# Attention with a quantized FFN between its pieces: the FFN's input ahead of the hidden rows on VectorE, its load and x1's load moved

## The chip, the cores and the metric

The kernel runs on one core of a Trainium2 chip. The metric is the time of the whole program on the device in microseconds (us). A core has TensorE (PE: matmuls and transposes by matmul), VectorE (DVE), ScalarE (ACT), GpSimd (POOL) and SyncE (SP), which here only issues DMAs. Each engine works through its own instructions in order and waits on semaphores for the others.

## The reference

All data are float32; x is 8 x 1024 x 512.

```python
def fp4_quant_dequant(x):            # blocks of 16 along the last axis
    scale = max(max(abs(block)) / 6, 1e-12)
    q = nearest of (0, .5, 1, 1.5, 2, 3, 4, 6) to abs(block / scale)
    return q * sign * scale

x = x + attention(layernorm(x))      # 16 heads, latent 128, rope, causal softmax
y = fp4(layernorm(x))
h = silu(y @ fp4(w_gate).T) * (y @ fp4(w_up).T)      # 1408 wide
x = x + fp4(h) @ fp4(w_down).T
```

## The kernel before

The attention is cut into 16 units, two per batch element, each of 512 query rows; an odd unit has more keys to go over than the even one before it. For every unit the latent projections are made, then the heads in four groups of four: scores on PE (`sc_ps`), the exponential on ACT (L597), clipping, masking and row sums on DVE and POOL, the sum over values on PE (`num`). The output projection of a unit (`po`, `out_proj`) comes in the next unit; DVE adds x (L772), and the result x1 goes to a DRAM buffer `mid`.

The FFN goes over 64 tiles n of 128 rows of x1. Its weights are quantized and turned once, in the first units. From the fifth unit on (about 553 us) the pieces of the FFN are laid between the steps of the attention, as fillers for PE; the last tiles stand alone at the end (from about 3640 us). For a tile n there are these pieces:

- `fetch(n)`: SP loads x1 into the tile `y` (one buffer).
- `begin(n)`: layernorm statistics (DVE L361 to L363, and a power on POOL), scaling (L367), then `quantize`: block maxima (L254), six small steps for the scales (L259 to L264, in `sc` and `rs`, one buffer each), and for each part of up to 512 columns a multiply (L281), a mask and a step size `m` (L289, L292; one buffer), an add and a subtract (L295) and a multiply (L277).
- `turned(n)`: four transposes of y on PE (L212), and ACT copies the result into `yT` (L214; two buffers).
- `gate(n, k)` and `up(n, k)`, k = 0, 1, 2: matmul groups of 512, 512 and 384 columns. ACT copies the gate into `h` (L142; two buffers) and makes the silu (L819); DVE multiplies by the up part (L831).
- After `up(n, 2)` `quantize` runs over h (1408 columns, three parts), each part ending in a transpose of 32 x 32 blocks (L218). `move_blocks` then issues sixteen DMAs on SP from h to `hT` (L230; one buffer), which finish the transpose.
- `down(n)`: matmuls of hT with the down weights into `pd`, DVE adds x1 (`xr`, in the three buffers of tag `xo`; L881), SP stores the rows. It stands in the program behind `gate(n + 2, 2)`.

The order on PE, DVE, ACT and SP is written out by the kernel itself (`tc.manual_schedule`); that of POOL is left to the scheduler. A planner, `Clock`, keeps an estimated time of PE, DVE and ACT. Work of DVE with no fixed place is queued as jobs with costs in `clk.soon` and `clk.later`; the FFN's quantizations go to `later`, one behind the other. `fill` takes jobs from the queues where DVE has time before its next fixed instruction; `need(key)` lays all jobs up to the last one of that key, just before PE depends on them. So `turned(n)` begins with `need(("y", n))` and `gate(n, 0)` with `need(("h", n - 2))`. Stores and the moves of h are kept back by `send` until the planner's time has come to their data.

The order of a tile's pieces is given by `ffn_pieces`; of before, it reads

```python
for k in range(3):
    yield (3.4, 3.4, 2.6)[k], n, lambda n=n, k=k: gate(n, k)
    if k < 2 and n < last:
        yield 0.0, n + 1, lambda n=n, f=(fetch, begin)[k]: f(n + 1)
```

so y of the next tile is loaded behind `gate(n, 0)` and begun behind `gate(n, 1)`, its jobs behind those of h of tile n - 1 that are still queued.

Of the kernel before, what the change touches and what calls it, by code (L numbers as in the profile page):

```python
# [11 lines left out]
F32 = mybir.dt.float32  # L12
U32 = mybir.dt.uint32
AF = mybir.ActivationFunctionType
ALU = mybir.AluOpType
# [3 lines left out]
P = 128  # L19
B, S, D = 8, 1024, 512  # L20
# [7 lines left out]
NDC = D // P  # L28
NFC = FF // P
BLK = 16  # L30
# [12 lines left out]
def tile_mla_then_fp4_ffn(  # L43
# [30 lines left out]


    ET = mybir.EngineType
    ctx.enter_context(tc.manual_schedule(engines={ET.PE, ET.DVE, ET.Activation, ET.SP}))

    class Clock:

# [18 lines left out]
                job[1]()  # L99

        def lay(self, q):
            cost, run, _, ready = q.popleft()
            self.dve = max(self.dve, ready) + cost
            run()

# [36 lines left out]
        on_act(0.1 + 0.0009 * src.free_size(), lambda: nc.scalar.copy(dst, src))  # L142

    def slack(cost, run, key, soon=False, ready=0.0):
        (clk.soon if soon else clk.later).append((cost, run, key, ready))

    ident = const.tile([P, P], F32, name="ident")
    make_identity(nc, ident)
# [68 lines left out]
    def turn_blocks(part, key, soon=False):  # L217
        slack(0.72, lambda: nc.vector.transpose(part, part), key, soon)  # L218
# [24 lines left out]
    BY_PE = (4 * 2 * B - 1,)  # L243


    def quantize(q, width, key):
        nb = width // BLK
        q3 = q.rearrange("p (b k) -> p b k", k=BLK)
        got = {}

        def amax():
            got["sc"] = sc = p1.tile([P, 88], F32, tag="sc", name="sc")[:, :nb]
            got["rs"] = rs = p1.tile([P, 88], F32, tag="rs", name="rs")[:, :nb]
            nc.vector.tensor_reduce(rs, q3, AX.X, ALU.max, apply_absolute_value=True)  # L254

        def scales():
            sc, rs = got["sc"], got["rs"]

            nc.vector.tensor_scalar(sc, rs, 1.0 / 6.0, None, ALU.mult)  # L259
            nc.vector.scalar_tensor_tensor(rs, sc, -4.0, rs, ALU.mult, ALU.add)  # L260
            nc.vector.scalar_tensor_tensor(rs, sc, -2.0, rs, ALU.mult, ALU.add)
            nc.vector.scalar_tensor_tensor(sc, rs, 1.0 / 6.0, sc, ALU.mult, ALU.add)
            nc.vector.tensor_scalar(sc, sc, 1e-12, None, ALU.max)
            nc.vector.reciprocal(rs, sc)  # L264

        slack(0.06 + 0.0011 * width, amax, key)
        slack(1.1 + 0.008 * nb, scales, key)
        for o in range(0, width, 512):
            step = min(512, width - o)
            part, bl = q[:, o : o + step], slice(o // BLK, (o + step) // BLK)  # L270
            nbl = step // BLK
            part3 = part.rearrange("p (b k) -> p b k", k=BLK)

            def times(which, part3=part3, bl=bl, nbl=nbl):
                by = got[which][:, bl].unsqueeze(2).to_broadcast([P, nbl, BLK])
                if which == "sc":
                    nc.vector.tensor_tensor(part3, part3, by, ALU.mult)  # L277
                else:


                    nc.vector.scalar_tensor_tensor(  # L281
                        part3, part3, BELOW_ONE, by, ALU.mult, ALU.mult
                    )

            def steps(part=part, step=step):
                got["m"] = m = p1.tile([P, 512], F32, tag="m", name="m")[:, :step]
                nc.vector.tensor_scalar(  # L289
                    m.bitcast(U32), part.bitcast(U32), EXP_MASK, None, ALU.bitwise_and  # L290
                )
                nc.vector.tensor_scalar(m, m, 1.0, MAGIC, ALU.max, ALU.mult)  # L292

            def to_grid(op, part=part):
                nc.vector.tensor_tensor(part, part, got["m"], op)  # L295

            pass_cost = 0.06 + 0.00125 * step
            slack(pass_cost, lambda f=times: f("rs"), key)
            slack(1.2 * pass_cost, steps, key)
            slack(pass_cost, lambda f=to_grid: f(ALU.add), key)  # L300
            slack(pass_cost, lambda f=to_grid: f(ALU.subtract), key)
            slack(pass_cost, lambda f=times: f("sc"), key)
            if key[0] == "h" and key[1] not in BY_PE:
                turn_blocks(part, key)


    def weight_pieces():
# [45 lines left out]
    def normed(xt, key):  # L353
        got = {}

        def stats():
            pool, tag = (small, "nx") if key[0] == "x" else (p1, "ny")
            own = pool.tile([P, 10], F32, tag=tag, name=tag)
            st, ve = own[:, 0:6], own[:, 8:9]
            got["mv"], got["rstd"] = mv, rstd = own[:, 6:8], own[:, 9:10]  # L360
            nc.vector.bn_stats(st, xt)  # L361
            nc.vector.bn_aggr(mv, st)
            nc.vector.tensor_scalar(ve, mv[:, 1:2], EPS, None, ALU.add)  # L363
            nc.gpsimd.tensor_tensor(rstd, ve, neg_half, ALU.pow)

        def scaled():
            nc.vector.tensor_scalar(  # L367
                xt, xt, got["mv"][:, 0:1], got["rstd"], ALU.subtract, ALU.mult
            )

        return [(0.9, stats, key), (0.5, scaled, key)]

    def begin_norms(jobs, soon=False):

        parts = [normed(*job) for job in jobs]
        for k in range(2):
            for part in parts:
                slack(*part[k], soon)
# [399 lines left out]


    tiles = [(u, t) for u in range(2 * B) for t in range(NT)]  # L780
    ys, hs, ends = {}, {}, {}

    def fetch(n):
        clk.sent_by_now("store")
        ys[n] = p1.tile([P, D], F32, tag="y", name=f"y_{n}")
        nc.sync.dma_start(out=ys[n], in_=mids[tiles[n]])

    def begin(n):
        begin_norms([(ys[n], ("y", n))])
        quantize(ys[n], D, ("y", n))  # L790

    def hidden(n, w, off, width):
        pg = bank("pg")[:, :width]
# [9 lines left out]

    def turned(n):
        clk.need(("y", n))
        yT = p2.tile([P, NDC, P], F32, tag="yT", name="yT")
        turn(ys[n], yT, NDC)
        ys[n] = yT

# [32 lines left out]
    def hidden_turned(n, done=None):  # L842

        if n in BY_PE:
            return
        if n > 0 and n - 1 not in used:
            waits[n] = clk.dve
            return
        h = hs.pop(n)

        def make():
            clk.sent_by_now("store")
            ends[n] = p3.tile([P, D], F32, tag="xo", name=f"xr_{n}")
            nc.sync.dma_start(out=ends[n], in_=mids.pop(tiles[n]))
            hTs[n] = p1.tile([P, NFC, P], F32, tag="hT", name="hT")
            return hTs[n]

        move_blocks(h, make, ("h", n), clk.dve if n == 0 or done is None else max(done, clk.pe))

    def down(n):  # L860
        clk.need(("h", n))
        if n in BY_PE:
            ends[n] = p3.tile([P, D], F32, tag="xo", name=f"xr_{n}")
            nc.sync.dma_start(out=ends[n], in_=mids.pop(tiles[n]))
            hTs[n] = p1.tile([P, NFC, P], F32, tag="hT", name="hT")
            for off, width in FCH:
                f0, c = off // P, width // P
                turn(hs[n][:, off : off + width], hTs[n][:, f0 : f0 + c, :], c)
            hs.pop(n)
        else:  # L870
            arrived(("h", n))
        hT = hTs[n]
        pd = bank("pd")
        for i in range(NFC):
            mm(pd, lhsT=hT[:, i, :], rhs=wd_T[:, i, :], start=(i == 0), stop=(i == NFC - 1))
        hTs.pop(n)
        used.add(n)
        if n + 1 in waits:
            hidden_turned(n + 1, waits.pop(n + 1))
        xt = ends.pop(n)  # L880
        on_dve(0.7, clk.pe + 0.3, lambda: nc.vector.tensor_tensor(xt, pd, xt, ALU.add))  # L881
        u, t = tiles[n]
        b, rows = rows_of(u, t)
        clk.send(clk.dve, lambda: nc.sync.dma_start(out=out[b, rows, :], in_=xt), "store")

    def ffn_pieces():

        last = len(tiles) - 1
        yield 4.0, 0, lambda: fetch(0)
        yield 10.0, 0, lambda: begin(0)  # L890
        yield 1.0, 0, lambda: turned(0)
        for n in range(last + 1):
            for k in range(3):
                yield (3.4, 3.4, 2.6)[k], n, lambda n=n, k=k: gate(n, k)
                if k < 2 and n < last:
                    yield 0.0, n + 1, lambda n=n, f=(fetch, begin)[k]: f(n + 1)
            if n > 1:
                yield 9.9, n, lambda n=n: down(n - 2)
            for k in range(3):
                yield (3.4, 3.4, 2.6)[k], n, lambda n=n, k=k: up(n, k)  # L900
                if k == 1 and n < last:
                    yield 0.5, n + 1, lambda n=n: turned(n + 1)
        for n in (last - 1, last):
            yield 9.9, last, lambda n=n: down(n)

# [135 lines left out]
```

## Time and profile before

| what | value |
|---|---|
| median of 3 runs | 3835.66 us (3835.64 to 3838.62) |
| the profiled execution, whole | 3835.01 us |
| its span, first to last instruction | 3833.3 us |
| mean granted TensorE clock | 0.974 |
| PE busy | 3559.1 us, 93% |
| DVE busy | 2873.8 us, 75% |
| ACT busy | 1145.5 us, 30% |
| POOL busy | 651.2 us, 17% |
| DVE waits for the loads of x at L772 | 113.4 us |

The profile is of one execution. Busy is the time in which an engine had an instruction under way. A wait is the idle time of an engine before an instruction, put down to the instruction or DMA that came last before it could start. "pt L212 <- DVE y L277" means: the instruction writing pt at line 212 waited for DVE's instruction at line 277, which wrote y. The granted clock is the share of full speed that TensorE was given; in windows of a few us it is near 1 or near 0.5.

### The profile page before, as it was taken

The numbers are of one execution on the slowest core, as the hardware profiler recorded it, in microseconds if no ns is written. First come the engines' busy times: TensorE is split into PE (matmuls) and PEld (weight loads), VectorE is DVE, ScalarE is ACT, GpSimd is POOL, SyncE is SP. The second block draws the span as 40 slices with busy tenths as digits, with TensorE's granted clock in tenths as the row PEclk, the third lists the DMA queues.
The fourth block names the chain that finished last, engine by engine and source line by source line (L and its number), as shares of the span: only waits on it lengthen the run. The fifth ranks groups of instructions, "written<-read, shape, count | busy, mean of one in ns | idle before, by whom it ended". The sixth has DMA issues, their size and how long they took to land. (4 is left out here: it accounts for less than half of the span.)

```text
span 3833.3 us, 45944 instructions
## 1 busy us (share of the span) xinstructions
PE 3559.1 (93%) x17119; PEld 1551.5 (40%) x17119; DVE 2873.8 (75%) x5024; ACT 1145.5 (30%) x1473; POOL 651.2 (17%) x838
## 2 busy tenths in 40 slices
PE   6998989999999998999999999989999999998898
PEld 3333334443444443344434444433444344433343
DVE  5886937777878777777778687776878786777776
ACT  2343433332323222232323233322323222232210
POOL 2233321111111111111111111111211111111100
PEclk9999999999999999999999999999999999999999
DMA  3212211311122211222111222112221113211221
GB/s 76 64 37 69 81 36 30 76 38 38 38 63 46 70 38 32 54 56 69 38 38 38 69 54 59 34 32 70 47 68 31 38 38 75 51 41 29 46 61 40
DMA packets 577038, 192.47 MB, mean 50 GB/s; under 512 B 514864, under 2 KB 515888, under 8 KB 576816
## 3 DMA queue, kind: packets, MB, share of 16 engines
q1 hardware_dynamic: 568512, 187.36, 21.0%
q10 hardware_dynamic: 8304, 2.18, 0.3%
q8 instruction: 136, 2.23, 0.2%
q14 instruction: 86, 0.70, 0.1%
HBM read 94.72 MB, written 33.55 MB: 33 GB/s over the span
## 5 line engine op out<-in xcount | busy, mean ns | idle before, releaser
L597 ACT ACTIVATE pT<-sc_ps 128x1024 f32<-128x1024 f32 (+1 forms) x640 | 566.1, 936 | 1174.6 <-PE sc_ps L129 964.6
L129 PE MATMUL pg<-wu_T,yT 128*128 128x512 f32 (+1 forms) x1536 | 669.2, 584 | 3.8 <-DVE xo L772 3.8
L129 PE MATMUL pg<-wg_T,yT 128*128 128x512 f32 (+1 forms) x1536 | 630.6, 561 | 0.7 <-ACT yT L214 0.7
L129 PE MATMUL pd<-wd_T,hT 128*128 128x512 f32 x1408 | 622.9, 598 | 4.4 <-DVE rs L264 4.4
L615 POOL TENSOR_SCALAR pT<-pT 128x1024 f32<-128x1024 f32 (+1 forms) x320 | 342.1, 1069 | 1065.4 <-ACT pT L597 847.6
L619 POOL TENSOR_SCALAR_AFFINE_SELECT pT<-pT 128x256 f32<-128x256 f32 (+1 forms) x384 | 233.4, 608 | 1462.6 <-DVE pT L612 1184.0
L641 DVE TENSOR_TENSOR pT<-pT 128x1024 f32<-128x1024 f32 (+3 forms) x528 | 472.7, 920 | 3.9 <-POOL pT L619 0.6
L129 PEld LDWEIGHTS pg<-wu_T,yT 128*128 128x128 f32 x1536 | 296.9, 200 | 333.9 <-issue 274.4
L129 PEld LDWEIGHTS pg<-wg_T,yT 128*128 128x128 f32 x1536 | 288.8, 190 | 326.1 <-issue 248.9
L129 PEld LDWEIGHTS pd<-wd_T,hT 128*128 128x128 f32 x1408 | 266.3, 191 | 345.5 <-issue 327.6
L612 DVE TENSOR_SCALAR pT<-pT 128x1024 f32<-128x1024 f32 (+1 forms) x320 | 205.0, 641 | 248.0 <-ACT pT L597 246.9
L129 PE MATMUL sc_ps<-qc,kT 32*128 32x512 f32 (+3 forms) x3072 | 343.5, 532 | 9.1 <-ACT pT L597 9.0
L129 PE MATMUL num<-pT,v 128*32 128x512 f32 (+3 forms) x3072 | 326.1, 501 | 5.6 <-POOL pT L619 5.2
L129 PE MATMUL sc_ps<-qr,kr 32*128 32x512 f32 (+3 forms) x3072 | 309.8, 488 | 4.2 <-DVE qr L533 4.2
L142 ACT COPY h<-pg 128x512 f32<-128x512 f32 (+1 forms) x192 | 105.7, 551 | 609.3 <-PE pg L129 580.6
L831 DVE TENSOR_TENSOR h<-pg,h 128x512 f32<-128x512 f32 (+1 forms) x192 | 123.1, 642 | 218.8 <-PE pg L129 208.3
L295 DVE TENSOR_TENSOR h<-h,m 128x512 f32<-128x512 f32 (+1 forms) x384 | 257.3, 670 | 11.8
L129 PE MATMUL po<-wo,aT 128*128 128x512 f32 x512 | 226.2, 600 | 30.9 <-DMA wo<-in_w_o_dram 27.9
L129 PEld LDWEIGHTS sc_ps<-qc,kT 32*128 32x128 f32 x3072 | 115.9, 186 | 226.8 <-issue 154.8
L212 PE MATMUL pt<-ident,y 128*128 128x128 f32 x256 | 48.2, 319 | 168.5 <-DVE y L277 158.1
L772 DVE TENSOR_TENSOR xo<-po,xo 128x512 f32<-128x512 f32 x64 | 44.1, 688 | 202.5 <-DMA xo<-in_x_dram 113.4
L129 PEld LDWEIGHTS sc_ps<-qr,kr 32*128 32x128 f32 x3072 | 147.3, 188 | 109.9 <-issue 85.5
(103 smaller groups left out, 3473.3 us busy)
## 6 DMA issues: line engine op xcount, KB each, us to landing
hT<-h SPq DMA_DIRECT2D x1008, 44.0 KB, 2.1
xo<-in_x_dram SPq DMA_DIRECT2D x64, 256.0 KB, 2.9
wo<-in_w_o_dram SPq DMA_DIRECT2D x16, 1024.0 KB, 5.2
mid<-xo SPq DMA_DIRECT2D x64, 256.0 KB, 2.8
y<-mid SPq DMA_DIRECT2D x64, 256.0 KB, 2.7
xr<-mid SPq DMA_DIRECT2D x64, 256.0 KB, 2.8
out_dram<-xr SPq DMA_DIRECT2D x64, 256.0 KB, 2.0
xp<-in_x_dram SPq DMA_DIRECT2D x30, 512.0 KB, 4.0
```

What stands on the lines that cost most here:

```text
L129: nc.tensor.matmul(dst, **kw)
L142: on_act(0.1 + 0.0009 * src.free_size(), lambda: nc.scalar.copy(dst, src))
L212: nc.tensor.transpose(pt[:, i, :], src[:, i * P : (i + 1) * P], ident)
L295: nc.vector.tensor_tensor(part, part, got["m"], op)
L597: lambda: nc.scalar.activation(part, sc[:, 2 * k : 2 * k + 2, :cols], AF.Exp, scale=SM_SCALE),
L612: lambda: nc.vector.tensor_scalar(part, part, E_HI, E_LO, ALU.min, ALU.max),
L615: nc.gpsimd.tensor_scalar(part, part, E_HI, E_LO, ALU.min, ALU.max)
L619: nc.gpsimd.affine_select(out=diag, in_=diag, pattern=[[0, 2], [0, len(segs)], [1, P]], compare_op=ALU.is_ge, fill=0.0, base=0, channel_mu ...
L641: lambda a=whole, b=part: nc.vector.tensor_tensor(a, a, b, ALU.add),
L772: on_dve(0.7, clk.pe + 0.3, lambda: nc.vector.tensor_tensor(xt, po, xt, ALU.add))
L831: lambda: nc.vector.tensor_tensor(h, pg, h, ALU.mult),
```

## The change

SP is no longer among the engines whose order is written out; the scheduler orders its DMAs. A job carries a flag that says whether others may be put in front of it (not where `m` is in use by the job before). `begin(n)` puts y's jobs in front of the first such job in `clk.later`, that is ahead of what is left of the hidden rows of earlier tiles, and y's scales are kept in the first columns of `yT`, which is now allocated there, in place of `sc` and `rs`. `begin(n + 1)` follows `gate(n, 0)` instead of `gate(n, 1)`; `fetch(n + 2)` follows `turned(n + 1)`, ahead of `up(n, 2)`, where before `fetch(n + 2)` stood behind `gate(n + 1, 0)`. `turned` also moves the planner's time of PE up to that of DVE. x1's load for the last add moves from the front of the sixteen DMAs of h into `down(n)`.

```diff
-    ctx.enter_context(tc.manual_schedule(engines={ET.PE, ET.DVE, ET.Activation, ET.SP}))
+    ctx.enter_context(tc.manual_schedule(engines={ET.PE, ET.DVE, ET.Activation}))
...
+    def ahead_of_rows(jobs):
+        q = clk.later
+        at = next((i for i, x in enumerate(q) if x[4]), len(q))
+        for job in reversed(jobs):
+            q.insert(at, (*job, 0.0, True))
...
-    def quantize(q, width, key):
+    def quantize_jobs(q, width, key, scales_in):
...
         def amax():
-            got["sc"] = sc = p1.tile([P, 88], F32, tag="sc", name="sc")[:, :nb]
-            got["rs"] = rs = p1.tile([P, 88], F32, tag="rs", name="rs")[:, :nb]
+            got["sc"], got["rs"] = sc, rs = scales_in()
...
+            jobs.append((pass_cost, lambda f=times: f("rs"), key, True))
+            jobs.append((1.2 * pass_cost, steps, key, True))
+            jobs.append((pass_cost, lambda f=to_grid: f(ALU.add), key, False))
+            jobs.append((pass_cost, lambda f=to_grid: f(ALU.subtract), key, False))
+            jobs.append((pass_cost, lambda f=times: f("sc"), key, True))
             if key[0] == "h" and key[1] not in BY_PE:
-                turn_blocks(part, key)
+                jobs.append((0.72, lambda p=part: nc.vector.transpose(p, p), key, True))
+        return jobs
...
     def begin(n):
-        begin_norms([(ys[n], ("y", n))])
-        quantize(ys[n], D, ("y", n))
+        yTs[n] = yT = p2.tile([P, NDC, P], F32, tag="yT", name="yT")
+        jobs = normed(ys[n], ("y", n))
+        scales_in = lambda: (yT[:, 0, : D // BLK], yT[:, 1, : D // BLK])
+        jobs += [x[:3] for x in quantize_jobs(ys[n], D, ("y", n), scales_in)]
+        ahead_of_rows(jobs)
...
     def turned(n):
         clk.need(("y", n))
-        yT = p2.tile([P, NDC, P], F32, tag="yT", name="yT")
+        clk.pe = max(clk.pe, clk.dve)
+        yT = yTs.pop(n)
...
         def make():
-            clk.sent_by_now("store")
-            ends[n] = p3.tile([P, D], F32, tag="xo", name=f"xr_{n}")
-            nc.sync.dma_start(out=ends[n], in_=mids.pop(tiles[n]))
             hTs[n] = p1.tile([P, NFC, P], F32, tag="hT", name="hT")
...
     def down(n):
         clk.need(("h", n))
+        clk.sent_by_now("store")
+        ends[n] = p3.tile([P, D], F32, tag="xo", name=f"xr_{n}")
+        nc.sync.dma_start(out=ends[n], in_=mids.pop(tiles[n]))
...
         yield 1.0, 0, lambda: turned(0)
+        yield 0.0, 1, lambda: fetch(1)
         for n in range(last + 1):
             for k in range(3):
                 yield (3.4, 3.4, 2.6)[k], n, lambda n=n, k=k: gate(n, k)
-                if k < 2 and n < last:
-                    yield 0.0, n + 1, lambda n=n, f=(fetch, begin)[k]: f(n + 1)
+                if k == 0 and n < last:
+                    yield 0.0, n + 1, lambda n=n: begin(n + 1)
...
                 if k == 1 and n < last:
                     yield 0.5, n + 1, lambda n=n: turned(n + 1)
+                    if n + 1 < last:
+                        yield 0.0, n + 2, lambda n=n: fetch(n + 2)
```

More of the change, by code (lines that the diff above doesn't have):

```diff
@@ L101, in lay @@
         def lay(self, q):
-            cost, run, _, ready = q.popleft()
+            cost, run, _, ready, _ = q.popleft()
             self.dve = max(self.dve, ready) + cost
@@ L144, in slack @@
     def slack(cost, run, key, soon=False, ready=0.0):
-        (clk.soon if soon else clk.later).append((cost, run, key, ready))
+        (clk.soon if soon else clk.later).append((cost, run, key, ready, True))
+    def ahead_of_rows(jobs):
[3 more added lines that the diff above has]
+            q.insert(at, (*job, 0.0, True))
     ident = const.tile([P, P], F32, name="ident")
@@ L243, in tile_mla_then_fp4_ffn @@
     BY_PE = (4 * 2 * B - 1,)
-    def quantize(q, width, key):
+    def quantize_jobs(q, width, key, scales_in):
         nb = width // BLK
         q3 = q.rearrange("p (b k) -> p b k", k=BLK)
-        got = {}
+        got, jobs = {}, []
         def amax():
-            got["sc"] = sc = p1.tile([P, 88], F32, tag="sc", name="sc")[:, :nb]
-            got["rs"] = rs = p1.tile([P, 88], F32, tag="rs", name="rs")[:, :nb]
+            got["sc"], got["rs"] = sc, rs = scales_in()
             nc.vector.tensor_reduce(rs, q3, AX.X, ALU.max, apply_absolute_value=True)
@@ L264, in scales @@
             nc.vector.reciprocal(rs, sc)
-        slack(0.06 + 0.0011 * width, amax, key)
-        slack(1.1 + 0.008 * nb, scales, key)
+        jobs.append((0.06 + 0.0011 * width, amax, key, True))
+        jobs.append((1.1 + 0.008 * nb, scales, key, True))
         for o in range(0, width, 512):
@@ L297, in quantize, with own @@
             pass_cost = 0.06 + 0.00125 * step
[L298 to L302, printed above, removed]
-            if key[0] == "h" and key[1] not in BY_PE:
-                turn_blocks(part, key)
+            jobs.append((pass_cost, lambda f=times: f("rs"), key, True))
[3 more added lines that the diff above has]
+            jobs.append((pass_cost, lambda f=times: f("sc"), key, True))
+            if key[0] == "h" and key[1] not in BY_PE:
+                jobs.append((0.72, lambda p=part: nc.vector.transpose(p, p), key, True))
+        return jobs
+    def quantize(q, width, key):
+        def own():
+            return [p1.tile([P, 88], F32, tag=x, name=x)[:, : width // BLK] for x in ("sc", "rs")]
+        for cost, run, k, free in quantize_jobs(q, width, key, own):
+            clk.later.append((cost, run, k, 0.0, free))
     def weight_pieces():
@@ L780, in tile_mla_then_fp4_ffn @@
     tiles = [(u, t) for u in range(2 * B) for t in range(NT)]
-    ys, hs, ends = {}, {}, {}
+    ys, yTs, hs, ends = {}, {}, {}, {}
     def fetch(n):
@@ L861, in down @@
         clk.need(("h", n))
+        clk.sent_by_now("store")
+        ends[n] = p3.tile([P, D], F32, tag="xo", name=f"xr_{n}")
+        nc.sync.dma_start(out=ends[n], in_=mids.pop(tiles[n]))
         if n in BY_PE:
-            ends[n] = p3.tile([P, D], F32, tag="xo", name=f"xr_{n}")
-            nc.sync.dma_start(out=ends[n], in_=mids.pop(tiles[n]))
             hTs[n] = p1.tile([P, NFC, P], F32, tag="hT", name="hT")
```

## The prediction

> **What bounds the kernel now.** I read the engines' busy time first, then TensorE's waits, then the stretch around one of its stalls on VectorE, TensorE, SyncE and ScalarE, and last the granted clock around a stall.
>
> The page's first part says which engine sets the time (busy us, share, instructions):
>
> ```profile
> span 3833.3 us, 45944 instructions
> PE 3559.1 (93%) x17119; PEld 1551.5 (40%) x17119; DVE 2873.8 (75%) x5024; ACT 1145.5 (30%) x1473; POOL 651.2 (17%) x838
> ```
>
> TensorE is busy 93% of the span and has some 270 us without work. That is all a new order can win, apart from clock. What it waits for (engine, line, releaser: total us, times, longest):
>
> ```profile
> PE pt L212 <- DVE y L277: 158.1, 40, 10.0
> PE po L129 <- DMA wo<-in_w_o_dram: 27.9, 8, 8.6
> ...
> PE pt L212 <- DVE xo L772: 10.4, 6, 2.6
> ...
> PE pv L129 <- DVE xr L881: 6.0, 5, 1.2
> PE pd L129 <- DVE rs L264: 4.4, 1, 4.4
> PE pg L129 <- DVE xo L772: 3.8, 4, 1.7
> ```
>
> Well over half of the idle time is one wait: the four transposes of an FFN input y need the last step of y's quantization (L277). By gaps of 0.8 us and more it is 156.5 us in 37 gaps; six gaps come back in every pair of attention units (a period of 522 us, five of them): 1.9, 5.7, 2.2, 7.4, 2.3 and 2.2 us, and the last tiles have 10.0, 6.3, 4.3, 7.3 and 2.2. The other lines are small.
>
> One of them, the 7.4 us, on VectorE, TensorE, SyncE and ScalarE (start, us, line, operation; the idle time before it in brackets):
>
> ```profile
> 1978.14 0.58 DVE L218 STREAM_TRANSPOSE h<-h 128x384 f32<-128x384 f32 x1
> ...
> 1981.94 0.68 DVE L361 BATCH_NORM_STATS2 ny<-y 128x6 f32<-128x512 f32 x1
> ...
> 1990.13 0.69 DVE L277 TENSOR_TENSOR y<-y,sc 128x512 f32<-128x512 f32 x1
> ```
> ```profile
> 1976.57 7.03 PE L129 MATMUL pg<-wu_T,yT 128*128 128x512 f32 x16
> 1990.97 1.08 PE L212 MATMUL pt<-ident,y 128*128 128x128 f32 x4 [7.37 <-DVE y L277]
> ```
> ```profile
> 1978.87 10.49 SPq L230 DMA_DIRECT2D hT<-h  x16
> 1992.09 0.33 SPq L786 DMA_DIRECT2D y<-mid  x1
> ```
> ```profile
> 2003.47 0.59 ACT L142 COPY h<-pg 128x512 f32<-128x512 f32 x1 [6.97 <-PE pg L129]
> ```
>
> VectorE never stood idle for long here. It finished the quantization of the previous h first, its last transpose ending at 1978.7, and only then began y, which took 1981.94 to 1990.82: 8.9 us, 0.7 of them a multiply of the path, so **y costs 8.2 us**. TensorE ended at 1983.6. SyncE started h's sixteen small DMAs at once and took 10.5 us to issue them; the last lands 2.1 us later by the page's DMA part, at about 1991.5. The copy that needs that h's buffer (two exist) starts at 2003.47, so **12 us were spare behind h** and none before y.
>
> **The change, part by part.** The program has as many instructions on each engine as before. TensorE's order is the same up to its 7893rd of 8769, and shifts in small pieces from tile 54 on. So the price is in waits.
>
> *y before the rows of h.* y's jobs enter the queue ahead of the previous tile's h, one matmul group (3.5 us at 16 per 7.03 us) earlier, with scales in a buffer of their own, so no wait for sc and rs. Following the built order tile by tile, with the durations of the rows, y comes too late on 40 tiles by 173 us in the order of before (156.5 were measured, so this way of counting is about 10% heavy), and in the changed order on one: tile 0, with 9.6 us, which has nothing earlier to go to. Every other tile has at least 16.9 us to spare. Gain: 156.5 - 9.6 = **147 us**. No cover is needed for that; the y that was late is simply not last. The bounds are 130 and 150.
>
> *The load of y a group sooner and x1's load beside down.* VectorE waits 113.4 us in all for x loads at L772, and TensorE 10.4 + 3.8 us behind that. With the x1 loads out of the way of the sixteen h DMAs these shrink, and I take the two TensorE rows, cut to 13.5 us by the same gap limit, as gone: **-13.5** (0 to -14). y's load is late by 4.4 us once per pair, hidden in the 16.9 us. x1's load takes 0.42 us of issue and 2.8 to land, and down's eleven weight tiles run about 9.7 us (622.9 us over 64 tiles), so it is covered; uncovered it would cost 64 x 3.2 = 205 us, but only on VectorE's last add, which no matmul needs but for its bank.
>
> *What is late next: h.* y's 8.2 us now stand before the rows of h. Those cost, per tile: maxima 1.6, scales 1.9, two wide parts of 0.69 + 0.51 + 0.54 + 2 x 0.70 + 0.76 + 0.71 = 4.6 each, one narrow part 3.6: 16.3 us. Behind them is the move: from the last transpose's end to the landing it took 12 to 12.7 us (10.5 to 11.4 of issue and 2.1). Only then may ScalarE copy gate(n+2, 0) into that h buffer, and it is in order: the exponentials of the attention, and so scores, are queued behind that copy. Counted along the built order with a move of 12.0 us, hT of tile n lands after gate(n+2, 0) is ready in six of ten tiles per pair, by 13.3, 7.3, 8.2, 6.0, 4.4 and 1.2 us. TensorE has work that does not need ScalarE for 4.3, 8.5, 6.1, 6.4, 8.3 and 7.6 us in those places; what is left is 9.0 + 0 + 2.1 + 0 + 0 + 0 = 11.1 us per pair, 55.5 in five. Tile 0 adds 13.9 - 8.3 = 5.6. In the end, without attention between, the loop is 8.2 + 16.3 + 12.0 us and some 3 us of multiplies and adds of the path, 39 to 40, against 30 us of TensorE work per tile; it is 6 to 13 us late on seven tiles and TensorE covers 5 to 7 of each: 23 us. Sum: 55.5 + 5.6 + 23 = **+84 us**. Before, ScalarE waited for hT 19.3 us in three places, all in the tail, and on the path it never did, so this wait is not shown by the trace at its new size. Lower bound 30 (only the tail and part of one tile per pair), upper bound 190 (4 us more per tile; one unlucky wait can do that, since SyncE itself was up to 14.5 us late with such a move in places). I take the count, as the move's duration is a measured one.
>
> *Other waits of the new VectorE order.* krp at L452 (0.4 us each) is found behind y on one group in each pair, **+13.5** in all (0 to 25). w_o's load is 4.8 us late per pair instead of 3.3: **+5** (0 to 40).
>
> *SyncE's order left to the scheduler.* In the built order the sixteen DMAs stand at most 0.6 us behind their transposes, where before they were held back 2.7 to 14.5 us on five tiles of the first pair; that is already in the numbers above. Stores move back, and nothing waits for them but their buffer. Taken as nothing beyond w_o; its price where it fails is a rival.
>
> *The clock.* A gap costs more than its length (columns: window, us; busy us and instructions of PE, PEld, DVE, ACT, POOL; granted clock; DMA share; GB/s):
>
> ```profile
> 1038.00:1042.30 4.30, 2.21 (x6) 0.66 (x4) 4.30 (x6) 0.00 (x0) 3.16 (x3) 1.00 0.14 21
> 1043.50:1047.00 3.50, 3.50 (x7) 1.68 (x5) 0.00 (x0) 0.14 (x1) 0.00 (x0) 0.51 0.65 225
> 1047.00:1050.40 3.40, 3.40 (x43) 1.81 (x43) 2.74 (x3) 1.51 (x2) 0.00 (x0) 1.00 0.00 0
> ```
>
> After a gap of 2.2 us the clock is 0.51 for 3.5 us, then full again. After the first 500 us TensorE is busy for 108 us at half clock, so 54 us are lost, over about 50 gaps: 1.1 us each. 42 gaps (37 + 5) go, some 24 come (two per pair, tile 0, seven in the tail, krp): 18 x 1.1 = **-20 us** (0 to -35). The Trainium skill ("TensorE: Matmul & The Clock Gate", "Part 1: The HAM clock gate") puts the half rate behind an idle window of about 3.4 us; the 2.2 us gap above speaks against this. By that rule the short gaps would have cost no clock, and the term would be an estimated -13, the sum -71.
>
> **Sum**, on the profiled execution (3835.0 us: the span of 3833.3 and 1.7 around it, 0.65 below the median): -147 - 13.5 + 84 + 13.5 + 5 - 20 = -78, that is **3757 us**.
>
> **Rivals.**
> *(1) Slower: the move of h becomes the bound.* Same mechanism as the +84, 4 us later on each tile that is late: then three more tiles per pair pass TensorE's cover and the stalls are 189 us instead of 84, with the clock's gain down to 5. 3835 + (-147 - 13.5 + 189 + 13.5 + 5 - 5) = **3877**. It turns the sign from about 3 us more per move (160 us of stalls eat the whole gain). For it: sixteen issues in a row of 10.5 to 11.4 us, and spare time of 6.8 to 17.5 us behind typical tiles, less than y's 8.2 for some. Against: the count already takes the slowest chain of each tile, and ran 10% heavy on the y waits. Chance 0.25.
> *(2) Slower: SyncE's order delays w_o or x.* If w_o comes 10 us later in each of the 11 units from 5 on, 110 us take the place of the 5: **3862**. For it: w_o's wait is 27.9 us already and its load goes behind everything issued before. Against: outside the first 550 us the row is only 13.7 us. Chance 0.06.
> *(3) Much faster: h's move is covered.* If ScalarE's copies wait but TensorE's scores always have a bank, -147 - 13.5 + 13.5 + 5 - 35 = -177: **3658**. For it: VectorE is 75% busy and waits 113 us for x alone. Against: ScalarE waits 6 to 7 us for hT in the tail even before. Chance 0.11.
> *(4) No difference within what a measurement can tell from none* (0.2%, 7.7 us): the stalls come out near 160. This is the border between the forecast and (1), chance 0.08.
>
> **How the numbers follow.** The forecast has 0.50; with (3), faster 0.61; (4) gives same 0.08; (1) and (2) give slower 0.31. The range reaches from 3685 (stalls near the lower bound of 30, clock -35) to 3882 (a little over rival 1): what lies under it is most of (3), above it the far end of (1). For the forecast alone it is 3715 to 3800.
>
> **What would show it.** Right: TensorE's wait for y at L277 falls to about 10 us in one place; the wait of ScalarE's copy L142 for hT rises from 19 us to over 100; the period of a pair goes from 522 to about 511 us; the granted clock rises above 0.974; VectorE's x waits shrink well below 113 us. Wrong: y still waits in many places (the reordering does not do what it says); TensorE idles behind ScalarE or hT for over 160 us; w_o's row grows beyond 40 us.

## The result, and the profile after

The changed kernel takes 3769.56 us (median of 4 runs, 3762.56 to 3771.3) against 3836.0 us: a ratio of 0.9822 (95% interval 0.9805 to 0.9839), 66 us less. The profiled execution took 3769.9 us. The profile's first part of the changed kernel:

```profile
span 3768.2 us, 45975 instructions
PE 3550.3 (94%) x17119; PEld 1550.3 (41%) x17119; DVE 2852.6 (76%) x5024; ACT 1136.8 (30%) x1473; POOL 669.8 (18%) x838
```

The span is 65.1 us shorter. TensorE's time without work (span less busy) fell from 274.2 to 217.9 us, and its busy time by 8.8 us with the same 17119 instructions, with the granted clock at 0.976 for 0.974. What TensorE now waits for:

```profile
PE pqr L129 <- ACT h L142: 41.9, 5, 9.0
PE sc_ps L129 <- ACT pT L612: 24.9, 22, 7.8
PE po L129 <- DMA wo<-in_w_o_dram: 24.5, 5, 13.2
...
PE pp L129 <- ACT h L142: 13.5, 5, 3.1
PE pp L129 <- DVE krp L467: 11.4, 6, 3.8
PE num L129 <- POOL pT L634: 11.2, 14, 1.5
PE pt L219 <- DVE y L284: 9.7, 1, 9.7
PE po L129 <- DVE aT L717: 8.5, 2, 4.3
```

The wait for y went from 158.1 us in 40 places to 9.7 in one. The new head of the list is ScalarE's copy of the gate into h. What that copy waits for is in ScalarE's waits, where the row was 19.3 us before:

```profile
ACT h L142 <- DMA hT<-h: 415.0, 31, 25.9
```

One place of the 41.9 us, once in every pair of units, on TensorE, ScalarE, SyncE and VectorE of the changed kernel:

```profile
1375.82 2.08 PE L129 MATMUL pqr<-cq,wqr 128*128 128x512 f32 x2 [8.32 <-ACT h L142]
```
```profile
1375.18 0.59 ACT L142 COPY h<-pg 128x512 f32<-128x512 f32 x1 [17.82 <-DMA hT<-h]
```
```profile
1362.98 10.51 SPq L237 DMA_DIRECT2D hT<-h  x16
```
```profile
1336.87 0.69 DVE L284 TENSOR_TENSOR y<-y,yT 128x512 f32<-128x512 f32 x1
...
1362.34 0.58 DVE L311 STREAM_TRANSPOSE h<-h 128x384 f32<-128x384 f32 x1
```

y was complete at 1337.6, h's last transpose only at 1362.9; sixteen issues and the landing took until 1375, and the copy that needs that buffer stood 17.8 us in ScalarE's order, TensorE 8.3 us behind it.

### The profile page after: what moved, and what is told of

It reads as the page before. It is cut to its first block, busy times and chain, and to the rows that moved or that the text cites. A ratio compares the mean times of both kernels' runs of the same rounds, so it can differ in the third digit from the quotient of the medians.

```text
span 3768.2 us, 45975 instructions
## 1 busy us (share of the span) xinstructions
PE 3550.3 (94%) x17119; PEld 1550.3 (41%) x17119; DVE 2852.6 (76%) x5024; ACT 1136.8 (30%) x1473; POOL 669.8 (18%) x838
## 4 chain that ended last, share of the span: by engine, by line
PE 58%; DVE 14%; SPq 6%; issue 3%; DMA 2%; ACT 2%; POOL 1%; DVEq 0%; ACTq 0%; POOLq 0%
PE pg L129 21%; PE pd L129 11%; PE sc_ps L129 8%; SPq L237 6%; PE po L129 5%; PE num L129 4%; PE pp L129 2%; DVE h L302 2%; DVE pT L656 2%; PE den L129 1%; DVE h L311 1%; DVE h L284 1%; DMA hT<-h 1%; PE pv L129 1%; PE pqr L129 1%
## 5 line engine op out<-in xcount | busy, mean ns | idle before, releaser
L129 PE MATMUL pg<-wg_T,yT 128*128 128x512 f32 (+1 forms) x1536 | 641.7, 569 | 2.4 <-ACT h L142 1.7
L129 PE MATMUL pg<-wu_T,yT 128*128 128x512 f32 (+1 forms) x1536 | 638.9, 562 | 0.0
L630 POOL TENSOR_SCALAR pT<-pT 128x1024 f32<-128x1024 f32 (+1 forms) x320 | 351.3, 1098 | 1049.1 <-ACT pT L612 677.4
L656 DVE TENSOR_TENSOR pT<-pT 128x1024 f32<-128x1024 f32 (+3 forms) x528 | 463.7, 904 | 3.7 <-POOL pT L634 0.6
L129 PEld LDWEIGHTS pg<-wu_T,yT 128*128 128x128 f32 x1536 | 282.6, 190 | 315.7 <-issue 248.7
L129 PE MATMUL sc_ps<-qc,kT 32*128 32x512 f32 (+3 forms) x3072 | 342.4, 530 | 25.0 <-ACT pT L612 24.9
L129 PE MATMUL num<-pT,v 128*32 128x512 f32 (+3 forms) x3072 | 327.8, 499 | 11.8 <-POOL pT L634 11.2
L129 PE MATMUL po<-wo,aT 128*128 128x512 f32 x512 | 236.5, 622 | 36.6 <-DMA wo<-in_w_o_dram 24.5
L302 DVE TENSOR_TENSOR h<-h,m 128x512 f32<-128x512 f32 (+1 forms) x384 | 260.1, 677 | 10.7
L129 PEld LDWEIGHTS po<-wo,aT 128*128 128x128 f32 x512 | 101.5, 200 | 169.2 <-issue 121.8
L129 PEld LDWEIGHTS num<-pT,v 128*32 128x32 f32 x3072 | 67.9, 108 | 224.8 <-issue 132.3
```

The source lines that it names most:

```text
L129: nc.tensor.matmul(dst, **kw)
L630: nc.gpsimd.tensor_scalar(part, part, E_HI, E_LO, ALU.min, ALU.max)
L656: lambda a=whole, b=part: nc.vector.tensor_tensor(a, a, b, ALU.add),
```

## The experiments

They ask which part of the change gives the gain, and what the wait for h costs. The theory going in (A) was the prediction's: the place in front of the rows of h gives nearly all, the move of h takes half of it back. Times are medians of four runs; the ratio is to the kernel before on the same chip.

**y_first_alone.** The kernel before with y's jobs in front, their scales in `yT`, and the change's line in `turned`; loads, places and SyncE's order are as before.

```diff
+        ahead_of_rows(jobs)          # y's jobs, scales in yT
```

> Kernel before with only y's jobs put in front of the rows of h (and y's scales in yT); pieces, x1's load and SyncE's order as before. Theory A (the order on VectorE carries nearly all the gain, the move of h the loss): TensorE's wait for y at L284 (L277 of before) falls from 158 to under 25 us, ScalarE's wait for hT rises to some hundred us, time 3755 to 3800. Theory B (the earlier load and start, or SyncE's free order, carry the gain): y still waits for over 80 us, time 3815 or more.

3888.51 us, ratio 1.0131 (1.0116 to 1.0147): slower than before. Neither theory gave this: TensorE's wait for y is 9.6 us, as A said, and the time is in B's range. VectorE's own waits show a row that before had not, and TensorE's have these, the first of which is 11.2 us in the changed kernel, where the second is missing:

```profile
DVE ny L376 <- DMA y<-mid: 175.9, 19, 12.5
```
```profile
PE num L129 <- POOL pT L634: 41.2, 19, 6.3
PE pg L129 <- DVE xr L901: 30.4, 6, 5.9
```

With y in front and its load still behind the sixteen DMAs of h, VectorE stands in order before y's statistics, and its later work with it. What TensorE loses by that is not h: its stalls behind the copies into h are 66 us here and 64 in the changed kernel. It is the rows behind xr (55 us for 7.5) and behind POOL's part of the attention, and the clock (TensorE's busy time is 3592.0 us for 3550.3). So the front place, without the rest of the change, is a loss.

**no_front.** The changed kernel without the front place:

```diff
-        ahead_of_rows(jobs)
+        for job in jobs:
+            clk.later.append((*job, 0.0, True))
```

> Changed kernel, but y's jobs go to the end of VectorE's queue, behind the rows of h, as before; the earlier load and start, x1's load beside down and SyncE's free order stay. Theory A: the y wait is back at 110 to 160 us, ScalarE's wait for hT falls below 100 us, time 3810 to 3850. Theory B: the y wait stays under 50 us, time 3755 to 3795.

3747.09 us, ratio 0.9764 (0.9747 to 0.978), 22 us *faster* than the changed kernel. That is under theory B's range, and A fell with it. TensorE's wait for y:

```profile
PE pt L219 <- DVE y L284: 96.1, 24, 9.6
```

62 of the 158 us of y's wait are gone without any change of order between y and h, and ScalarE has no row for hT. The same place as above, in no_front:

```profile
1359.42 1.12 PE L219 MATMUL pt<-ident,y 128*128 128x128 f32 x4 [5.70 <-DVE y L284]
```
```profile
1338.92 10.51 SPq L237 DMA_DIRECT2D hT<-h  x16
```

Here h's move starts some 22 us earlier in the program's course than above (24 on the clock; ScalarE's copy of qc lies at 1353.8 here and at 1356.3 there) and nobody waits for it; y is late by 5.7 us. In the changed kernel y is in time and h costs 8.3. VectorE is short by 6 to 8 us at this point of the pair, and the order only chooses who pays. From here on I had a theory H in place of A: the earlier start of y carries the gain (early_alone below says how far that held); the front place moves VectorE's shortage from y to h, where it is paid through the move.

**plain4.** The changed kernel with a shorter move, four DMAs in place of sixteen; it leaves out the exchange of the 32 x 32 blocks:

```diff
-                for q in range(4):
-                    nc.sync.dma_start(
-                        out=dst[32 * q : 32 * q + 32, :, 32 * g : 32 * g + 32],
-                        in_=src4[32 * g : 32 * g + 32, q])
+                nc.sync.dma_start(
+                    out=dst[32 * g : 32 * g + 32].rearrange("p n k -> p (n k)"),
+                    in_=src[32 * g : 32 * g + 32])
```

> Changed kernel with the move of h done by four plain DMAs in place of sixteen: same bytes, same place in the order, but the exchange of the 32 x 32 blocks is left out. The move takes about 5 us instead of 12. Theory A (the loss is h's lateness by its move): six of ten tiles land 7 us earlier, only one per pair is still late by 2 us beyond TensorE's cover, stalls behind ScalarE's copy of h fall from some 80 to 10 to 20 us, time 3690 to 3712. Theory C (the stalls come from VectorE's own order, the move is only the last in the chain's record): they stay over 55 us, time 3745 or more.

3642.85 us, ratio 0.9492 (0.9478 to 0.9507): 127 us under the changed kernel, some 50 more than A's range. TensorE's busy time and its wait behind the copy into h:

```profile
PE 3517.4 (97%) x17119; PEld 1536.1 (42%) x17119; DVE 2855.2 (78%) x5024; ACT 1140.6 (31%) x1473; POOL 665.6 (18%) x838
```

```profile
PE pqr L129 <- ACT h L142: 10.0, 5, 2.4
```

The copy's wait did fall as A said. What was left out of the expectation: the waits for krp (11.4 to 3.8 us) and aT went too (that they were late behind the same stalls is likely, not shown), and TensorE's busy time fell by 33 us with the clock at 0.988.

**move_plus.** The changed kernel with six DMAs of each move issued twice:

```diff
+            if key[0] == "h":
+                for q in range(6):
+                    nc.sync.dma_start(... the block (q % 4, 3) again ...)
```

> Changed kernel with six of the sixteen DMAs of each move issued twice, to the same places with the same data: each move 3.7 to 4.3 us longer. Theory A (the slower rival of the prediction priced it): stalls behind hT rise by about 105 us and the clock loses some 10, time 3850 to 3890. Theory C: TensorE's other work covers it, time below 3800.

3962.52 us, ratio 1.0328 (1.0313 to 1.0344): 193 us more than the changed kernel, where some 100 was expected. In the profiles TensorE lost 151 us more to idleness and 39.5 us more to the clock (busy 3589.8 for 3550.3). With plain4 this prices a microsecond of the move: about 18 us of time per us taken off (127 for some 7), some 48 per us put on (193 for 4).

**no_front_plain4.** The two edits of no_front and plain4 together.

> As no_front (y behind the rows of h), with the move of h by four plain DMAs, the exchange of the 32 x 32 blocks left out. Theory H (with y in front VectorE's shortage falls on h and is paid through the move; with y behind it falls on y, and the move has slack): the edit that gave 127 us in the changed kernel gives little here, time 3725 to 3750, y's wait stays at 85 to 100 us. If the move's length is a cost in any order (DMA queues, SyncE): below 3700.

3746.54 us, ratio 0.9758 (0.9744 to 0.9773): no difference to no_front's 3747.09; the y wait is 96.2 us. The edit that gave 127 us with y in front gives nothing with y behind. H holds: the length of the move is a cost only because of the front place.

**act_half.** A shorter move that computes everything:

```diff
-                    nc.sync.dma_start(
+                    (nc.scalar if key[0] == "h" and q in (1, 3) else nc.sync).dma_start(
```

> Changed kernel with eight of the sixteen DMAs of each move issued by ScalarE instead of SyncE, the same work, the result complete. The move takes about 7 us instead of 12 if the issues run side by side; ScalarE pays about 5 us of issue per tile and may stand waiting for the transposes. Theory A (the move's length is the loss): stalls behind hT fall to 20 to 50 us, time 3680 to 3740. If ScalarE's wait in its order costs more than the shorter move gives: 3770 or more.

3764.11 us, ratio 0.9805 (0.9788 to 0.9821), the same as the changed kernel within the intervals, and between the two expectations. The two queues did work side by side (5.3 us of issue on SyncE, 5.6 on ScalarE, from the same moment), and TensorE's row of 41.9 us fell to 18.8. But ScalarE now stands before its own DMAs for the transposes: its waits "<- DMA hT<-h" before exponentials and copies of the attention come to some 300 us, and on TensorE the rows of pv (24.1 us for 7.5), of pg (29 for 2.4) and of po behind w_o (39.7 for 24.5) grew.

**sp_manual, late_places, xr_early.** Three parts of the change undone, one at a time, in the changed kernel:

```diff
# sp_manual
-    ctx.enter_context(tc.manual_schedule(engines={ET.PE, ET.DVE, ET.Activation}))
+    ctx.enter_context(tc.manual_schedule(engines={ET.PE, ET.DVE, ET.Activation, ET.SP}))
# late_places: fetch(n + 1) behind gate(n, 0), begin(n + 1) behind gate(n, 1)
# xr_early: xr's load in make(), in front of the sixteen DMAs
```

> Changed kernel with SyncE's order written by the planner again; all else as changed. Theory D (SyncE's free order starts h's move right behind its transposes): the moves start later by up to 14 us in places, ScalarE's wait for hT (415 us) and TensorE's stalls behind it grow, time 3790 to 3840. Theory E (with the loads placed earlier the written order is as good): 3760 to 3780.

3804.92 us, ratio 0.9912 (0.9897 to 0.9927): 35 us slower than with the free order. The way expected for it was wrong, though: ScalarE's wait for hT did not grow (380 us for 415). The row that grew is another (11.2 us with the free order):

```profile
PE num L129 <- POOL pT L634: 37.4, 20, 5.7
```

Why POOL gets late with SyncE's written order was not tried.

> Changed kernel with the load and the start of y back at their places of before (load behind gate(n, 0), start behind gate(n, 1)); y still in front of the rows of h, SyncE free, x1's load beside down. Theory F (y in front needs the earlier load, or VectorE stands before y's statistics and h with it): VectorE's wait for y's load rises from 38 us to over 100, time 3800 to 3890. Theory G (what made y_first_alone slow is SyncE's written order alone): that wait stays under 60 us, time 3755 to 3785.

3769.37 us, ratio 0.9816 (0.9801 to 0.9831): no change. VectorE's wait for y's load is 45.2 us (38.5 in the changed kernel). So F falls: with SyncE free and y in front, the earlier places add nothing. G holds in this much, that the free order, with x1's load in `down(n)`, takes away what made y_first_alone slow. The written order alone did not make it so: sp_manual has that order too, with the earlier places and x1's load in `down(n)`, and there the wait is 63.6 us instead of 175.9 and the time 84 us less. Which of those two helps there was not tried.

> Changed kernel with x1's load back in front of the sixteen DMAs of h. Theory D: in SyncE's order that load, and its wait for a free buffer of tag xo, can hold up the move; h later by 0.5 to 3 us on late tiles, time 3770 to 3830. If x1's load has no part in it: 3760 to 3775.

3769.97 us, ratio 0.9821 (0.9802 to 0.984): no change. With SyncE free, where x1's load stands does not matter.

**sp_free_alone and early_alone.** The two candidates for the gain, without the front place: the kernel before with SyncE free, and the changed kernel with neither the front place nor SyncE free.

> Kernel before with only SyncE's order left to the scheduler. If that order by itself gives much of the gain: TensorE's waits behind xo at L772 (14 us) go and VectorE's wait for x (113 us) falls below 50, y's wait (158 us) falls below 130, time 3790 to 3815. If it helps only beside the earlier pieces: y's wait stays at 150 or more, time 3820 to 3840.

> Changed kernel with y's jobs behind the rows of h and SyncE's order written by the planner: what is left of the change is the earlier load and start of y and x1's load beside down. If the earlier start carries the gain of the kernel without the front place (92 us): y's wait 90 to 110 us, time 3750 to 3785. If it is the free order: y's wait over 130 us, time 3800 to 3835.

sp_free_alone: 3818.67 us, ratio 0.9949 (0.9932 to 0.9965). early_alone: 3744.79 us, ratio 0.9757 (0.9743 to 0.9772), as fast as no_front. The y wait of the first and of the second:

```profile
PE pt L212 <- DVE y L277: 158.2, 40, 10.0
```
```profile
PE pt L219 <- DVE y L284: 96.0, 24, 9.6
```

The free order alone gives 18 us and leaves y's wait; TensorE's waits behind xo (14 us) are what went. In early_alone they went too (1.0 us left), and there the free order gives nothing more (no_front). So what else the change holds gives 92 us alone. That is a bundle: the earlier load and start of y, x1's load in `down(n)`, the scales in `yT`, and the line in `turned` that moves the planner's time of PE.

Within it, the earlier start is not what TensorE gained by in the five pairs, where some 45 of the 62 us lie (107.7 to 62.2). One place where the wait went, with h's last transpose and the start of y on VectorE and y's transposes on TensorE, first in the kernel before, then in early_alone:

```profile
1406.46 0.57 DVE L218 STREAM_TRANSPOSE h<-h 128x384 f32<-128x384 f32 x1
1406.95 0.65 DVE L361 BATCH_NORM_STATS2 ny<-y 128x6 f32<-128x512 f32 x1
```
```profile
1417.89 0.66 PE L212 MATMUL pt<-ident,y 128*128 128x128 f32 x4 [2.19 <-DVE y L277]
```
```profile
1381.49 0.58 DVE L311 STREAM_TRANSPOSE h<-h 128x384 f32<-128x384 f32 x1
1381.99 0.65 DVE L376 BATCH_NORM_STATS2 ny<-y 128x6 f32<-128x512 f32 x1
```
```profile
1398.97 0.60 PE L219 MATMUL pt<-ident,y 128*128 128x128 f32 x4
```

In both, y begins at the end of h's last transpose, and its load was issued long before that (36 and 27 us); the kernel before has no wait of VectorE for that load at all. What came sooner is h: y's transposes on TensorE start 11.4 us after that last transpose in the kernel before, with a wait of 2.2 us, and 17.5 us after it in early_alone, with none. VectorE took up h's rows earlier, ahead of fixed work of the attention. This is what the line in `turned` does: the planner's PE is later, so `fill` sees more time before the next fixed instruction and lays more jobs there. Read off the programs, and not run: early_alone without this line has VectorE's order of the kernel before from tile 2 to tile 53, and with the line but y's load and start at their old places it keeps its own there. In the last tiles, with some 17 of the 62 us, the line and the places both change the order, and their shares were not taken apart. So the first half of H was right in that the gain needs no front place, and wrong in its cause.

**front_some.** What H points to: y in front only where, in the traces of no_front and of the changed kernel, y's lateness costs more than h's.

```diff
-        ahead_of_rows(jobs)
+        if n == 2 or (n < 54 and n % 10 in (8, 0)):
+            ahead_of_rows(jobs)
+        else:
+            for job in jobs:
+                clk.later.append((*job, 0.0, True))
```

> Changed kernel with y in front of the rows of h only at tile 2 and, up to tile 53, at those tiles of each ten where y was later without it than h is with it (the 8th and 0th), elsewhere behind. Theory H: the y waits left are the 5.7 us ones per pair, tile 0 and the end, some 52 us; stalls behind h 10 to 20 us; time 3710 to 3740, below both kernels and no_front (3747). If one place in front disturbs its neighbours: 3745 to 3770.

3721.38 us, ratio 0.9697 (0.9682 to 0.9711), the fastest kernel that computes everything: 116 us under the kernel before on its chip, 48 under the changed one.

```profile
PE pt L219 <- DVE y L284: 53.3, 13, 9.6
PE pp L129 <- ACT h L142: 15.3, 5, 4.3
```

y's wait is what was expected; the wait behind h came back in one place per pair. The choice fits this kernel's period of ten tiles and no other.

## Why the prediction came out, point by point

The time (3757 forecast, 3769.6 measured) and most terms held, and so did the signs that the prediction named: a pair takes some 510 us for 522 (511 forecast). The reasons given for two terms did not hold, and the clock was mis-sized. Rows without a term took some 9 us, the largest TensorE's num behind POOL (5.2 to 11.2 us).

*y, -147.* Measured -148.4 (158.1 to 9.7), with tile 0 left as said. But the prediction gave it all to the order in front of h. The runs split it: the rest of the change takes 62 us at no price, some 45 of them by where the planner lays the rows of h; the front place takes the other 86 and is the sole reason for the next term. The line in `turned` had no term in the prediction, and the term came out near all the same because with y in front y is in time, whichever part is credited with it.

*h, +84.* Stalls behind the copy and hT: 41.9 + 13.5 + 5.3 + 2.0 + 1.7 in the rows of "ACT h", and 15.9 more of sc_ps behind ScalarE than before (24.9 less 9.0), 80 us. The place was right too: ScalarE's copy in its order, two places per pair (8.1 to 9.0 and 2.3 to 3.1 us, where 9.0 and 2.1 stood). The step that failed is the one that was not taken: the prediction set +84 against -147 as prices of the whole change, and never set the front place's own 86 against its own 80, plus krp and clock. Done so, the front place is a loss, which no_front shows by 22 us.

*x and x1, -13.5.* The rows of TensorE behind xo did go. The cause given, x1's load out of the way, is not needed for it: xr_early puts it back without effect, and sp_free_alone removes the rows alone. Under SyncE's written order it may still be the cause, as early_alone, which has that order, is rid of the rows too. VectorE's wait for x fell from 113.4 to 26.4 us, as said it would, but in early_alone it is still 101.2 and the time is 92 us down: that wait was no measure of the gain.

*krp, +13.5 and w_o, +5.* krp measured +11.4. po's rows (w_o, aT, h and rc together) went from 30.9 to 36.6 us: +5.7, though of w_o's load itself nothing (27.9 to 24.5).

*SyncE's order, taken as nothing.* Alone it is worth 18 us, with the front place 35, with the rest of the change but not the front place nothing. That it should cost (rival 2) was not seen in any run.

*The clock, -20.* Measured -8.8. It was counted by gaps: 18 fewer at 1.1 us each. By the same limit of 0.8 us there were 14 fewer after the first 500 us (58 to 44), and the price per gap does not hold: no_front has 24 fewer and gains 10.7 us of busy time, plain4 36 fewer and gains 41.7. Around the 8.3 us gap shown above (window, us; busy of PE, PEld, DVE, ACT, POOL; granted clock; DMA share; GB/s):

```profile
1372.00:1375.80 3.80, 0.00 (x0) 0.00 (x0) 0.00 (x0) 0.62 (x2) 0.00 (x0) 0.50 0.44 65
1377.00:1381.00 4.00, 4.00 (x6) 1.52 (x5) 3.56 (x7) 0.74 (x2) 2.86 (x4) 0.50 0.32 50
1381.00:1384.50 3.50, 3.50 (x11) 1.79 (x10) 3.23 (x10) 0.59 (x1) 0.00 (x0) 0.99 0.30 47
```

Over 5 us of work at half rate follow this gap, where 3.5 followed the one of 2.2 us: gaps are not all alike, and these were longer. In the kernel before, half rate follows the 2.2 us gaps of two places in all five pairs (those from 894.0 and 1040.2 us on in the first), and none follows the 2.26 us gap of each pair (the clock is 1.00 from 1518.5 to 1524 us, after one of them) nor the six of 2.5 to 3.3 us. So neither one price per gap nor a gap's length alone gives the term. Working by the Trainium skill ("TensorE: Matmul & The Clock Gate", Part 1), which asks for a whole idle window, the term was an estimated -13 and nearer; the 2.2 us gap still contradicts its limit, so no count is shown to be right.

*Rival 1.* Its mechanism is the real one, but its price was too low. move_plus is its case, 4 us more per move: 3963 us where it said 3877, 151 us more idleness instead of 105 and 39.5 us of clock instead of 15. At 48 us per us the sign would turn at an estimated 1.4 us more per move (66 / 48), not 3. The forecast stood closer to the edge than it said. *Rival 3* (h's move covered, 3658 us) is close to what plain4 shows, 3643, with a move made shorter instead of covered.

## What to carry to other kernels

When two jobs on one busy engine both feed the bound engine, putting one first does not remove the shortage, it picks who is late; price the loss of the job put back, with all that hangs behind it (here a move of 12 us), against the gain of that one edit, not against the gain of the whole change. Laying the jobs into time that the engine had unfilled, with their order kept, had no such price here, and belongs in its own line of the sum. Where a change has several parts, each needs a term of its own, a single line in a planner too: here the parts around the front place gave more than the whole, and the front place took some back. A job that begins at the end of the one before it is not helped by an earlier load or an earlier place in the queue; look first at what it stands behind.

## What the runs showed of the hardware

A DMA of the 44 KB move takes SyncE about 0.62 us to issue (the median in the changed kernel), and sixteen took 10.5 us in the place above; with half of them on ScalarE's queue the two ran side by side (5.3 and 5.6 us, act_half). TensorE's busy time for the same 17119 instructions ran from 3517.4 us (plain4, mean clock 0.988) to 3592.0 (y_first_alone, 0.963): 75 us that no wait's row shows.
